# First batches of TensorE written out by hand, one step less between down and up products, W1 on two DMA queues

## The chip, the cores and the metric

The kernel runs on one core of a Trainium2 chip. The metric is device time in microseconds (us) of one execution. Three runs of the kernel before gave 326.95, 327.93 and 328.11 us, median 327.93.

A core has five engines that run side by side and wait for each other through semaphores: TensorE (PE; its weight loads are shown apart as PEld), VectorE (DVE), ScalarE (ACT), GpSimd (POOL) and SyncE (SP), which here only issues DMAs. Each engine takes its instructions in the order of its own list.

## What is computed

128 batches of a 128 x 512 float32 matrix `x[b]`, each with a language id that picks one of ten sets of weights. In the reference, cut to what matters (`_L0_cond_ref` gets `x` as `hidden_states` and the ids as `language_ids`):

```python
w1 = W1[language_ids]; w2 = W2[language_ids]        # (512,128) and (128,512) of each batch
h = relu(einsum('bsh,bha->bsa', hidden_states, w1) + b1[language_ids][:, None, :])
adapted = einsum('bsa,bah->bsh', h, w2) + b2[language_ids][:, None, :]
x = hidden_states + adapted
mean = jnp.mean(x, axis=-1, keepdims=True)
var = jnp.mean(jnp.square(x - mean), axis=-1, keepdims=True)
normed = (x - mean) * rsqrt(var + 1e-5)
return normed * gamma[language_ids][:, None, :] + beta[language_ids][:, None, :]
# and the result is the original x plus this
```

## The kernel before

**Start.** All ten W1, all ten W2 and the rows of beta, gamma and b2 are loaded once. SP issues, in this order: the ids, gamma, the first half of x group 0 (`load_part(0, 2)`, L83), four slices of W1 (L93, 640 KB each, `k` in 0..3), the second half of x group 0, W2 in two halves (L98), and x groups 1 and 2 (L67, `load_x`; a group is four batches, 1 MB). ACT issues beta, b2 and b1.

The thirty rows (ten each of beta, gamma, b2) must stand on all 128 partitions. `spread(r)` does one row: a TensorE product (L155) that picks row `r` out of three stacked bf16 parts into a PSUM buffer of pool `p_y`, and a copy (about 0.6 us) out of it, on ACT where `r % 3 == 2` (L158) and on DVE otherwise (L160). The pool `p_y` has five buffers, used in turn, and the up products take theirs from it too.

**A batch** passes through these functions: `transpose_x` (PE, four 128 x 128 transposes into the single buffer of `p_x`, L191), `copy_xT` (ACT, L195), `stage_w1` (ACT copies the batch's W1 so that TensorE can read it at a fixed address, L186), `down` (PE, four products into the single buffer of `p_h`, L214), `relu` (ACT, L222, reads `p_h`), `up` (PE, L231, with one more product, L230, that adds b2 where `b2_by_matmul`), `residual` (DVE, L237), `negative_mean` (DVE), `square` and `deviation` (ACT), `rstd_1` to `rstd_5`, `scale` and `finish` (DVE, L281 and L290), `store` (SP). POOL prepares `x + b2` (`add_b2`, L201) and `x + beta` (`add_beta`, L208).

**Order.** `keep` ties each engine's instructions to the order in which the program calls them, so the order is written out by hand: one loop over steps `i`. Step `i` has the transposes of batch `i`, the down product of `i-1`, the up product of `i-U` and the residual of `i-U-1`. U is 3. The first `F = U+1 = 4` steps also issue 7 or 8 spreads each, after the step's down product, and hold back the up products; at step 4 come `down(3)`, `up(0)` and `up(1)` ahead of the transposes of batch 4. Fourteen products on a tile of ones (`idle`, L307) stand ahead of everything on TensorE.

`lid` loads the ids of a group of four batches into an engine's registers (L168) when it is first called for that group and engine. At the end of a step it is called ahead for a coming batch.

Of the kernel before, what the change touches and what calls it, by code (L numbers as in the profile page):

```python
# [8 lines left out]
FP = mybir.dt.float32  # L9
BF = mybir.dt.bfloat16  # L10
I32 = mybir.dt.int32
AF = mybir.ActivationFunctionType
# [4 lines left out]
P = 128  # L17
G = 4
EPS = 1e-5
U = 3  # L20


@with_exitstack
def cond_resid_kernel(ctx: ExitStack, tc: tile.TileContext, x, itok, W1, b1, W2, b2, gamma, beta, out):
# [8 lines left out]
    nc = tc.nc  # L33
    B, S, H = x.shape
    L, _, A = W1.shape
# [7 lines left out]
    def keep(ins):  # L43

        engine = ins.ins.engine
        if engine in last:
            tc.add_manual_dep(ins.ins, last[engine], behind, reason="kept order")
        last[engine] = ins.ins.name
        return ins

    const = ctx.enter_context(tc.tile_pool(name="const", bufs=1))
# [6 lines left out]
    p_x = ctx.enter_context(tc.tile_pool(name="p_x", bufs=1, space=PSUM))  # L58
    p_h = ctx.enter_context(tc.tile_pool(name="p_h", bufs=1, space=PSUM))
    p_s = ctx.enter_context(tc.tile_pool(name="p_s", bufs=1, space=PSUM))  # L60
# [4 lines left out]
    def load_x(g):  # L65
        t = xp.tile([P, G, H], FP, tag="x", name=f"x_{g}")
        keep(nc.sync.dma_start(out=t, in_=x[g * G : (g + 1) * G].rearrange("b s h -> s b h")))  # L67
        xs[g] = t

    def xb(b):  # L70
        return xs[b // G][:, b % G, :]
# [5 lines left out]
    w1 = const.tile([P, L, KC, A], FP, name="w1")  # L77
# [4 lines left out]
    def load_part(lo, hi):  # L82
        keep(nc.sync.dma_start(out=x_0[:, lo:hi, :], in_=x[lo:hi].rearrange("b s h -> s b h")))  # L83
# [4 lines left out]
    keep(nc.scalar.dma_start(out=rows[2 * L : 3 * L, :], in_=b2))  # L88
    load_part(0, 2)
    keep(nc.scalar.dma_start(out=b1r, in_=b1))  # L90
    for k in range(KC):
        keep(
            nc.sync.dma_start(out=w1[:, :, k, :], in_=W1[:, k * P : (k + 1) * P, :].rearrange("l p a -> p l a"))  # L93
        )
    load_part(2, G)
    for l in range(0, L, 5):
        keep(
            nc.sync.dma_start(  # L98
                out=w2[:, l * H : (l + 5) * H].rearrange("p (l h) -> p l h", l=5),
                in_=W2[l : l + 5].rearrange("l a h -> a l h"),  # L100
            )
        )
    for g in range(1, 3):
        load_x(g)

    warm = const.tile([P, 1], FP, name="warm")
    nc.vector.memset(warm, 1.0)
    keep(nc.scalar.activation(warm, warm, AF.Sqrt))

    ident = const.tile([P, P], FP, name="ident")  # L110
    make_identity(nc, ident)
# [2 lines left out]
    ones = const.tile([P, P], BF, name="ones")  # L114
# [10 lines left out]
    R = 3 * L  # L125
# [15 lines left out]
    def transpose_b1():  # L141
        b1p = p_h.tile([P, P], FP, tag="h", name="b1p")
        keep(nc.tensor.transpose(b1p[:, :L], b1r, ident[:L, :L]))
        keep(nc.vector.tensor_copy(b1T, b1p[:, :L]))
# [3 lines left out]
    gamma_b = const.tile([P, L * H], FP, name="gamma_b")  # L148
    b2_b = const.tile([P, L * H], FP, name="b2_b")

    def spread(r):
        t = (beta_b, gamma_b, b2_b)[r // L]
        row = p_y.tile([P, H], FP, tag="y", name=f"row_{r}")
        pick_r = pick[:, r : r + 1].to_broadcast([96, P])
        keep(nc.tensor.matmul(row, lhsT=pick_r, rhs=parts[:96, :], start=True, stop=True))  # L155
        dst = t[:, r % L * H : (r % L + 1) * H]
        if r % 3 == 2:
            keep(nc.scalar.copy(dst, row))  # L158
        else:
            keep(nc.vector.tensor_copy(dst, row))  # L160

    lids, xT, w1s, hT, rs, os, ys, ssqs, nmeans, rstds = {}, {}, {}, {}, {}, {}, {}, {}, {}, {}
    phs, pxs, sums = {}, {}, {}

    def lid(b, engine):
        g = b // G
        if (g, engine) not in lids:
            loads, vals = nc.values_load_multi_w_load_instructions(  # L168
                lang[0:1, g * G : (g + 1) * G],
                engines=[engine],  # L170
                min_val=0,
                max_val=L - 1,
                skip_runtime_bounds_check_because="clamped on the chip to 0..L-1 above",
            )
            for ins in loads:
                keep(ins)
            lids[g, engine] = vals
        return lids[g, engine][b % G]

    def b2_by_matmul(b):  # L180
        return b < 4 or b % 4 == 1

    def stage_w1(b):
        w1s[b] = wp.tile([P, KC, A], FP, tag="w1s", name=f"w1s_{b}")
        src = w1.rearrange("p l k a -> p (l k a)")[:, bass.ds(lid(b, ET.Activation) * (KC * A), KC * A)]
        keep(nc.scalar.copy(w1s[b].rearrange("p k a -> p (k a)"), src))  # L186

    def transpose_x(b):
        pxs[b] = p_x.tile([P, KC, P], FP, tag="xT", name=f"pxT_{b}")
        for k in range(KC):  # L190
            keep(nc.tensor.transpose(pxs[b][:, k, :], xb(b)[:, k * P : (k + 1) * P], ident))  # L191

    def copy_xT(b):
        xT[b] = tp.tile([P, KC, P], FP, tag="xT", name=f"xT_{b}")
        keep(nc.scalar.copy(xT[b], pxs.pop(b)))  # L195
# [14 lines left out]
    def down(b):  # L210
        phs[b] = p_h.tile([P, P], FP, tag="h", name=f"ph_{b}")
        for k in range(KC):
            keep(
                nc.tensor.matmul(  # L214
                    phs[b], lhsT=w1s[b][:, k, :], rhs=xT[b][:, k, :], start=(k == 0), stop=(k == KC - 1)
                )
            )
        del xT[b], w1s[b]

    def relu(b):  # L220
        hT[b] = tp.tile([P, P], FP, tag="hT", name=f"hT_{b}", bufs=6)
        keep(nc.scalar.activation(hT[b], phs.pop(b), AF.Relu, bias=b1T[:, bass.ds(lid(b, ET.Activation), 1)]))  # L222

    def up(b):
        v = lid(b, ET.PE)
        ys[b] = p_y.tile([P, H], FP, tag="y", name=f"py_{b}")
        m = b2_by_matmul(b)
        if m:
            pick_b = pick[:, bass.ds(v + 2 * L, 1)].to_broadcast([96, P])
            keep(nc.tensor.matmul(ys[b], lhsT=pick_b, rhs=parts[:96, :], start=True, stop=False))  # L230
        keep(nc.tensor.matmul(ys[b], lhsT=hT[b], rhs=w2[:, bass.ds(v * H, H)], start=not m, stop=True))  # L231
        del hT[b]
# [29 lines left out]
    def rstd_2(g):  # L262
        y0s[g] = st.tile([P, 2], FP, tag="y0", name=f"y0_{g}")
        keep(nc.vector.reciprocal(y0s[g], sds.pop(g)))
# [32 lines left out]
    def on(b):  # L297
        return 0 <= b < B
# [3 lines left out]
        nc.sync.dma_start(out=out[b], in_=os[g][:, j, :])  # L302


    idle = p_x.tile([P, H], FP, tag="xT", name="idle")
    for _ in range(14):
        keep(nc.tensor.matmul(idle, lhsT=ones, rhs=ones[:, 0:1].to_broadcast([P, H]), start=True, stop=True))  # L307

    F = U + 1
    for i in range(B + U + 7):  # L310
        if i < B and i % G == 0 and i // G + 3 < NG:
            load_x(i // G + 3)
        b = i - U - 1
        if i == F:
            down(i - 1)
            up(0)
            up(1)
        if on(i):
            transpose_x(i)
        if i == 0:  # L320
            transpose_b1()
        if on(b + 2):
            add_b2(b + 2)
        if on(b):
            add_beta(b)
        if on(i - 1) and i != F:
            down(i - 1)
        if on(i):
            copy_xT(i)
        if i < F:  # L330
            if on(i - 1):
                relu(i - 1)
            for r in range(i * R // F, (i + 1) * R // F):
                spread(r)
            if i == 0:
                stage_w1(0)
            stage_w1(i + 1)
        else:
            if on(i + 1):
                stage_w1(i + 1)  # L340
            if on(i - 1):
                relu(i - 1)
        if i > F and on(i - U):
            up(i - U)


        g, half = divmod(b, 2)
        p = g - 1
        mine, old = 0 <= p < B // 2, 0 <= p - 1 < B // 2
        if half == 0:  # L350
            if on(b):
                residual(b)
            if mine:
                scale(2 * p)
            if on(b):
                negative_mean(b)
            if mine:
                rstd_1(p)
                rstd_2(p)
            if old:  # L360
                finish(2 * p - 1)
                if p < B // 2:
                    store(p - 1)
                else:
                    store_half(B - 1)
            if mine:
                rstd_3(p)
        else:
            if on(b):
                residual(b)  # L370
            if mine:
                rstd_4(p)
                scale(2 * p + 1)
                rstd_5(p)
            if on(b):
                negative_mean(b)
            if mine:
                finish(2 * p)
                if p == B // 2 - 1:
                    store_half(B - 2)  # L380
        if on(b):
            square(b)
            if half == 1:
                deviation(g)

        for n, engine in ((i + 3, ET.Activation), (i - U + 3, ET.PE), (b + 1, ET.DVE), (b + 5, ET.Pool)):
            if on(n):
                lid(n, engine)
# [37 lines left out]
```

## Time and profile before

| | |
|---|---|
| median of three runs | 327.93 us |
| the profiled execution | 327.5 us |
| its span, first to last instruction | 325.7 us |
| PE, DVE, ACT, POOL busy | 304.6, 301.5, 283.6, 274.7 us |
| mean granted TensorE clock | 0.972 |
| bytes moved by DMA | 72.88 MB |

The profiled execution lasted 1.8 us longer than its span, and lies 0.4 us under the median. Busy times are of records that overlap a little where an engine is pipelined, so a stage with "40.00 of 40.00" says that no gap is seen, not that the engine could do no more. A timeline line gives the start, the length, the engine and line, and in brackets the idle time ahead of it with what ended it.

### The profile page before, as it was taken

The page shows a single profiled execution, that of the slowest core. Times are in us where ns is not written, and L with a number is a line of the kernel's source. Part 1 is how long each engine was busy: PE and PEld are TensorE (multiplying, and loading weights), DVE is VectorE, ACT ScalarE, POOL GpSimd, SP SyncE. Part 2 cuts the span into 40 slices and gives each one's busy share as a digit, 9 for nine tenths or more (in the row PEclk, how much of TensorE's full clock was granted, in tenths as well). Part 3 has the DMA queues.
Part 4 walks back from the last instruction along what each step waited for, and adds up shares of the span by engine and source line. Part 5 has one row for each costly group of instructions (what it writes and reads, how often), then busy time and mean ns, then how long its engine had stood idle before and what let it go on. Part 6 is the DMA issues. An engine that isn't in the chain of part 4 may idle for free. (4 is left out here: it accounts for less than half of the span.)

```text
span 325.7 us, 7127 instructions
## 1 busy us (share of the span) xinstructions
PE 304.6 (94%) x1872; PEld 225.4 (69%) x1872; DVE 301.5 (93%) x993; ACT 283.6 (87%) x716; POOL 274.7 (84%) x229
## 2 busy tenths in 40 slices
PE   8298999999999999999999999999999999999940
PEld 3255777877777777777777787777777877777710
DVE  6267699999999999999999999999999999999995
ACT  3266999999999999999999999999999999999940
POOL 1034989999999999999999999999999999999910
PEclk9679999999999999999999999999999999999995
DMA  7996296666666777766666667777666666733323
GB/s 209 322 387 252 48 332 222 223 219 225 233 244 224 236 258 262 253 213 214 208 233 241 235 223 255 259 251 237 222 220 222 230 232 227 233 132 130 129 115 144
DMA packets 40954, 72.88 MB, mean 224 GB/s; under 512 B 1705, under 2 KB 6836, under 8 KB 40914
## 3 DMA queue, kind: packets, MB, share of 16 engines
q1 hardware_dynamic: 40854, 72.38, 66.0%
q8 instruction: 15, 0.25, 0.3%
q14 instruction: 25, 0.20, 0.2%
q10 hardware_dynamic: 60, 0.05, 0.1%
HBM read 38.86 MB, written 33.55 MB: 222 GB/s over the span
## 5 line engine op out<-in xcount | busy, mean ns | idle before, releaser
L208 POOL TENSOR_TENSOR o<-x,beta_b 128x512 f32<-128x512 f32 x128 | 162.0, 1278 | 17.6 <-DVE beta_b L160 17.6
L214 PE MATMUL ph<-xT,w1s 128*128 128x128 f32 x1024 | 136.4, 276 | 5.8 <-ACT w1s L186 5.6
L201 POOL TENSOR_TENSOR r<-x,b_b 128x512 f32<-128x512 f32 x93 | 118.8, 1277 | 17.3 <-DVE py L237 10.1
L231 PE MATMUL py<-w,hT 128*128 x256 | 131.2, 594 | 1.9 <-ACT sq L249 1.3
L214 PEld LDWEIGHTS ph<-xT,w1s 128*128 128x128 f32 x1024 | 125.4, 193 | 7.1 <-ACT w1s L186 5.9
L191 PEld LDWEIGHTS pxT<-ident,x 128*128 128x128 f32 x512 | 64.0, 141 | 68.3 <-issue 41.2
L281 DVE SCALAR_TENSOR_TENSOR py<-py,nmean,gamma_b 128x512 f32<-128x512 f32 x128 | 96.2, 751 | 0.0
L290 DVE SCALAR_TENSOR_TENSOR o<-py,rstd,o 128x512 f32<-128x512 f32 x128 | 94.7, 740 | 1.5 <-issue 0.4
L249 ACT ACTIVATE sq<-py,nmean 128x512 f32<-128x512 f32 x128 | 88.4, 690 | 5.5 <-DVE nmean L242 5.0
L195 ACT COPY xT<-pxT 128x512 f32<-128x512 f32 x128 | 74.6, 583 | 14.2 <-PE pxT L191 10.3
L186 ACT COPY w1s<-w 128x512 f32 x128 | 80.0, 626 | 5.5 <-DMA w<-in_L_cond_W_dram 5.5
L191 PE MATMUL pxT<-ident,x 128*128 128x128 f32 x512 | 77.3, 274 | 1.0 <-ACT xT L195 0.7
L237 DVE SCALAR_TENSOR_TENSOR py<-py,r 128x512 f32<-128x512 f32 x93 | 64.5, 694 | 2.4 <-PE pxT L191 0.7
L222 ACT ACTIVATE hT<-ph,b1T 128x128 f32<-128x128 f32 x128 | 48.1, 376 | 2.0 <-PE ph L214 1.9
L231 PEld LDWEIGHTS py<-w,hT 128*128 128x128 f32 x256 | 41.6, 192 | 5.2 <-ACT sq L249 2.1
L237 DVE SCALAR_TENSOR_TENSOR py<-py,x 128x512 f32<-128x512 f32 x35 | 24.2, 692 | 4.7 <-PE py L231 3.9
L249 ACT ACTIVATION_READ_ACCUMULATOR sq<-py,nmean 128x1 f32 x128 | 26.3, 205 | 0.0
L255 ACT ACTIVATE sd<-ssq,eps 128x2 f32<-128x2 f32 x64 | 18.9, 296 | 2.1
L242 DVE TENSOR_SCALAR nmean<-sum 128x1 f32<-128x1 f32 x128 | 18.7, 146 | 0.1
L230 PE MATMUL py<-parts,pick 96*128 96x512 bf16 x35 | 13.3, 381 | 0.0
L270 DVE TENSOR_TENSOR stat<-stat,y 128x2 f32<-128x2 f32 x64 | 13.2, 206 | 0.0
L237 DVE DVE_READ_ACCUMULATOR py<-py,r 128x1 f32 x93 | 13.1, 141 | 0.0
(41 smaller groups left out, 92.7 us busy)
## 6 DMA issues: line engine op xcount, KB each, us to landing
out_dram<-o SPq DMA_DIRECT2D x63, 512.0 KB, 3.5
x<-in_x_dram SPq DMA_DIRECT2D x31, 1024.0 KB, 6.1
w<-in_L_cond_W_dram SPq DMA_DIRECT2D x4, 640.0 KB, 6.3
w<-in_L_cond_W_dram SPq DMA_DIRECT2D x2, 1280.0 KB, 11.4
x<-in_x_dram SPq DMA_DIRECT2D x2, 512.0 KB, 3.6
out_dram<-o SPq DMA_DIRECT2D x2, 256.0 KB, 2.1
rows<-in_L_cond_beta_dram ACTq DMA_DIRECT2D x1, 20.0 KB
rows<-in_L_cond_gamma_dram SPq DMA_DIRECT2D x1, 20.0 KB
```

Source lines behind the costliest of these rows:

```text
L186: keep(nc.scalar.copy(w1s[b].rearrange("p k a -> p (k a)"), src))
L191: keep(nc.tensor.transpose(pxs[b][:, k, :], xb(b)[:, k * P : (k + 1) * P], ident))
L195: keep(nc.scalar.copy(xT[b], pxs.pop(b)))
L201: keep(nc.gpsimd.tensor_tensor(rs[b], xb(b), b2_b[:, bass.ds(v * H, H)], ALU.add))
L208: keep(nc.gpsimd.tensor_tensor(os[g][:, j, :], xb(b), beta_b[:, bass.ds(v * H, H)], ALU.add))
L214: nc.tensor.matmul(phs[b], lhsT=w1s[b][:, k, :], rhs=xT[b][:, k, :], start=(k == 0), stop=(k == KC - 1))
L222: keep(nc.scalar.activation(hT[b], phs.pop(b), AF.Relu, bias=b1T[:, bass.ds(lid(b, ET.Activation), 1)]))
L231: keep(nc.tensor.matmul(ys[b], lhsT=hT[b], rhs=w2[:, bass.ds(v * H, H)], start=not m, stop=True))
L237: keep(nc.vector.scalar_tensor_tensor(ys[b], ys[b], 1.0, r, ALU.mult, ALU.add, accum_out=s))
L249: keep(nc.scalar.activation(sq, ys[b], AF.Square, bias=nmeans[b], accum_out=ssqs[g][:, j : j + 1]))
L281: nc.vector.scalar_tensor_tensor(ys[b], ys[b], nmeans.pop(b), gamma_b[:, bass.ds(v * H, H)], ALU.add, ALU.mult)
L290: nc.vector.scalar_tensor_tensor(o, ys.pop(b), rstds[g][:, j : j + 1], o, ALU.mult, ALU.add)
```

## The change

1. U goes from 3 to 2: the up product of batch `b` is issued in step `b+2`, and with it all that follows a batch, one step sooner after its transposes.
2. The slices `k` = 2 and 3 of W1 are issued by ACT, behind its table load and a small activation, which now come first on it; SP issues `k` = 0 and 1.
3. x group 3 is loaded with groups 1 and 2; before, step 0 of the loop issued it, at the same place of SP's order.
4. TensorE's first four batches are written out ahead of the loop, which now begins at step 3. The order on TensorE is: 12 products on ones (14 before); the transposes of batch 0; rows 0 to 5; the transposes of batch 1; rows 6 to 21, each followed by a half-width product on ones (`spin(1, H // 2)`, 16 in all); four full-width ones; then `down(0)`, transposes of 2, rows 22 to 24, `down(1)`, transposes of 3, rows 25 to 27, `down(2)`, rows 28 and 29, `up(0)`, `up(1)`, `down(3)`, `up(2)`, transposes of 4. Before, it was: transposes of 0, seven rows, transposes of 1, `down(0)`, eight rows, transposes of 2, `down(1)`, seven rows, transposes of 3, `down(2)`, eight rows, `down(3)`, `up(0)`, `up(1)`, transposes of 4.
5. The products on ones write a tile of pool `p_s` and no longer one of `p_x`.
6. Rows 22 to 29 are all copied by DVE: 7 row copies on ACT and 23 on DVE, where it was 10 and 20. `stage_w1(0)` and `stage_w1(1)` stand on ACT behind all seven.

```diff
-U = 3
+U = 2
...
+    warm = const.tile([P, 1], FP, name="warm")
+    nc.vector.memset(warm, 1.0)
+    keep(nc.scalar.activation(warm, warm, AF.Sqrt))
     for k in range(KC):
+        queue = nc.sync if k < 2 else nc.scalar
         keep(
-            nc.sync.dma_start(out=w1[:, :, k, :], in_=W1[:, k * P : (k + 1) * P, :].rearrange("l p a -> p l a"))
+            queue.dma_start(out=w1[:, :, k, :], in_=W1[:, k * P : (k + 1) * P, :].rearrange("l p a -> p l a"))
         )
...
-    for g in range(1, 3):
+    for g in range(1, 4):
         load_x(g)
-
-    warm = const.tile([P, 1], FP, name="warm")
-    nc.vector.memset(warm, 1.0)
-    keep(nc.scalar.activation(warm, warm, AF.Sqrt))
...
-    def spread(r):
+    def spread(r, copier):
...
-        if r % 3 == 2:
+        if copier is nc.scalar:
...
-    idle = p_x.tile([P, H], FP, tag="xT", name="idle")
-    for _ in range(14):
-        keep(nc.tensor.matmul(idle, lhsT=ones, rhs=ones[:, 0:1].to_broadcast([P, H]), start=True, stop=True))
-
-    F = U + 1
-    for i in range(B + U + 7):
+    def spin(n, width):
+        idle = p_s.tile([P, H], FP, tag="s", name="idle")
+        for _ in range(n):
+            keep(
+                nc.tensor.matmul(
+                    idle[:, :width], lhsT=ones, rhs=ones[:, 0:1].to_broadcast([P, width]), start=True, stop=True
+                )
+            )
+
+
+    spin(12, H)
+    transpose_x(0)
+    transpose_b1()
+    copy_xT(0)
+    for r in range(22):
+        spread(r, nc.scalar if r % 3 == 2 else nc.vector)
+        if r == 5:
+            transpose_x(1)
+            copy_xT(1)
+        elif r > 5:
+            spin(1, H // 2)
+    stage_w1(0)
+    stage_w1(1)
+    spin(4, H)
+    for b in range(3):
+        down(b)
+        if b < 2:
+            transpose_x(b + 2)
+        relu(b)
+        if b < 2:
+            copy_xT(b + 2)
+        for r in range(22 + 3 * b, min(25 + 3 * b, R)):
+            spread(r, nc.vector)
+        stage_w1(b + 2)
+    up(0)
+    up(1)
+    down(3)
+    relu(3)
+    stage_w1(5)
+
+    for i in range(3, B + U + 7):
...
-        if i == F:
-            down(i - 1)
-            up(0)
-            up(1)
-        if on(i):
+        if i == 4:
+            up(2)
+        if i > 3 and on(i):
             transpose_x(i)
...
-        if on(i - 1) and i != F:
+        if i > 4 and on(i - 1):
             down(i - 1)
-        if on(i):
+        if i > 3 and on(i):
             copy_xT(i)
-        if i < F:
...
+        if i > 4 and on(i + 1):
             stage_w1(i + 1)
-        else:
...
-        if i > F and on(i - U):
+        if i > 4 and on(i - 1):
+            relu(i - 1)
+        if i > 4 and on(i - U):
             up(i - U)
```

More of the change, by code (lines that the diff above doesn't have):

```diff
@@ L313, in cond_resid_kernel @@
         b = i - U - 1
-        if i == F:
-            down(i - 1)
-            up(0)
-            up(1)
-        if on(i):
+        if i == 4:
+            up(2)
+        if i > 3 and on(i):
             transpose_x(i)
-        if i == 0:
-            transpose_b1()
         if on(b + 2):
@@ L325, in cond_resid_kernel @@
             add_beta(b)
-        if on(i - 1) and i != F:
+        if i > 4 and on(i - 1):
             down(i - 1)
-        if on(i):
+        if i > 3 and on(i):
             copy_xT(i)
-        if i < F:
[L331 to L336, printed above, removed]
-            stage_w1(i + 1)
-        else:
[L339 to L342, printed above, removed]
-        if i > F and on(i - U):
+        if i > 4 and on(i + 1):
+            stage_w1(i + 1)
+        if i > 4 and on(i - 1):
+            relu(i - 1)
+        if i > 4 and on(i - U):
             up(i - U)
```

## The prediction

> **What bounds the kernel now.** First the busy time of each engine by stage (windows view; columns in the header line):
>
> ```profile
> core 0: us, PE busy (x) PEld busy (x) DVE busy (x) ACT busy (x) POOL busy (x), PEclk, DMA share, GB/s
> 40.00:80.00 40.00, 40.00 (x254) 30.30 (x254) 39.65 (x136) 38.26 (x99) 37.98 (x31) 1.00 0.73 247
> ...
> 280.00:310.00 30.00, 30.00 (x192) 22.77 (x190) 29.76 (x100) 28.41 (x74) 29.22 (x24) 1.00 0.36 141
> ```
>
> From 40 us to 310 us TensorE has no gap, at full clock. DVE is close behind. In the PE timeline the transposes of batch 6 start at 34.35 and those of batch 127 at 306.25: 271.90 / 121 = 2.247 us a batch. DVE alone, once TensorE is done, takes 2.21 (residuals at 311.12 and 315.54, two batches apart). So TensorE sets the pace and DVE has 0.04 us a batch to spare. What is won before the steady stretch is carried to the end if TensorE and DVE both get it. The tail is DVE's: `residual(124)` starts at 308.94, right after `up(124)`, and DVE then hardly stops until 322.16.
>
> The start is different (PE timeline; batches are told apart by the order of the list):
>
> ```profile
> 1.17 4.50 PE L307 MATMUL idle<-ones 128*128 128x512 bf16 x14 [1.17 <-POOL ones L115]
> ...
> 8.56 0.63 PE L191 MATMUL pxT<-ident,x 128*128 128x128 f32 x4 [0.20 <-PE row L155]
> 14.82 2.08 PE L214 MATMUL ph<-xT,w1s 128*128 128x128 f32 x8 [5.63 <-ACT w1s L186]
> 16.69 3.62 PE L155 MATMUL row<-parts,pick 96*128 96x512 bf16 x8
> ...
> 30.15 0.60 PE L191 MATMUL pxT<-ident,x 128*128 128x128 f32 x4
> 31.48 0.65 PE L191 MATMUL pxT<-ident,x 128*128 128x128 f32 x4 [0.73 <-ACT xT L195]
> ...
> 35.90 1.02 PE L231 MATMUL py<-w,hT 128*128 x2
> ```
>
> TensorE stands still for 5.63 us for the W1 copy of `down(0)`, and then is slow: that product takes 2.08 us where it takes 1.06 later, eight rows 3.62 where later 2.13. The windows view says why:
>
> ```profile
> 10.00:12.00 2.00, 0.00 (x0) 0.00 (x0) 0.00 (x0) 0.00 (x0) 0.00 (x0) 0.66 1.20 290
> 12.00:14.00 2.00, 0.00 (x0) 0.00 (x0) 0.00 (x0) 0.00 (x0) 0.00 (x0) 0.50 1.16 307
> ...
> 16.00:18.00 2.00, 2.00 (x9) 1.11 (x8) 0.64 (x1) 0.58 (x2) 0.00 (x0) 0.50 1.05 388
> ...
> 22.00:24.00 2.00, 1.78 (x9) 0.82 (x8) 1.76 (x3) 1.56 (x4) 0.00 (x0) 1.00 1.04 386
> ```
>
> From 10 us to almost 21 us the granted clock is half. And while TensorE, DVE and ACT all stand still (10 to 14 us), 23 of the 30 rows are yet to be spread. ACT and SP show what they wait for:
>
> ```profile
> 14.15 1.14 ACT L186 COPY w1s<-w 128x512 f32 x2 [5.48 <-DMA w<-in_L_cond_W_dram]
> ```
>
> ```profile
> 1.95 6.11 SPq L93 DMA_DIRECT2D w<-in_L_cond_W_dram x4
> 8.11 2.20 SPq L83 DMA_DIRECT2D x<-in_x_dram x1
> 10.35 1.65 SPq L98 DMA_DIRECT2D w<-in_L_cond_W_dram x2
> ```
>
> W1 lands just before 14.15. The landing records put the W2 halves at 18.66 and 22.22 and x group 1 at 24.75. Last, DVE gets its third up product late, 3.31 us after it could take it:
>
> ```profile
> 34.60 0.70 DVE L237 SCALAR_TENSOR_TENSOR py<-py,x 128x512 f32<-128x512 f32 x1 [3.31 <-PE py L231]
> ```
>
> [...] idle from 9.1, half clock from about 10.6, full again near 20.9. [...] Before, W1 moves at 290 to 307 GB/s with a DMA share of 1.16 to 1.20: the engines are full[...]; two queues are not shown before. [...]
>
> **The change part by part**, against the profiled 327.5 us (span 325.7).
>
> *W1 on two queues: 0.* The 2.62 MB lie behind the same full engines. ACT issues at about 3.6 (its activation ends at 3.56); SP's first two issues took 0.46 and 0.66 us, so ACT is free near 4.8, ahead of its first copy at about 5.9. Bounds: if two queues raised the rate to the 387 GB/s of the later stretch, W1 would land 2 us sooner; if ACT's slices only get short turns beside SP's x and W2, up to 2 us later; if ACT is held in issuing as SP was on its third slice (2.67 us), all ACT's copies slip by 1 to 2 us. W2 and x follow the same sum of bytes, so 22.2 and 24.75 stay. x group 3 keeps its place on SP.
>
> *Rows ahead of `down(0)`.* Of rows 0 to 21 DVE copies 15, at 0.62 us (five took 3.08), from 6.92 on: to 16.2. ACT copies seven in its shadow. A row's product needs the buffer of the row five before it, so row 20 is issued when row 15, DVE's 11th, is out: 6.92 + 11 x 0.62 = 13.7; ACT copies it by 14.8. TensorE's own pace, a row (0.25) and a half-width product (estimate 0.15, from half of 0.22 and its load), is 1.2 us per three rows against DVE's 1.24: even. Row 21 is out at about 14.5, the four full products end at 15.5. `stage_w1(0)` runs on ACT from 14.8, W1 being there. So `down(0)` starts at 15.5 to 16.5 (before: 14.82), at full clock, with 22 rows done and not 7. The 28 products on ones that stand behind or between rows cost nothing while DVE's copies or W1 cover them; uncovered, about 1 us. Two fewer at the head: 0.4 us, covered by DVE's preparation of the rows (first row at 6.5).
>
> *From `down(0)` to the transposes of 4*, from starts in the timeline at full clock: down 0.90, transposes 0.43, row 0.25, up with b2 1.08. Down, transposes, three rows, twice: 4.2. `down(2)` and two rows: 1.4. That gives `up(0)` at 21.1 or later, but W2's second half is only there at 22.2: its second product starts near 22.3 and ends at 23.2. This wait is the new limit. Behind it on TensorE stand `up(1)` 1.08, `down(3)` 0.90, `up(2)` 1.08, with a load of ids into registers ahead of the last (0.33): the transposes of 4 start at 26.2 to 26.6 (before: 30.15), just after x group 1.
>
> *Then ACT.* It has `relu(3)`, `stage_w1(5)` and `square(0)` ahead of `copy_xT(4)`, so that copy ends near 27.4, and the transposes of 5 start at 27.5 to 28 (before: 31.48, with the same wait). `down(4)` and `up(3)` follow: `up(3)` ends near 30. Before it ended at 36.76. **Gain about 6.8**, of which 1.3 (transposes and a down product) come from U, as up products no longer stand behind one more batch.
>
> *U = 2 in the steady stretch: 0.* `up(i-2)` stands right behind `down(i-1)`, which writes the single `p_h` buffer and so waits for `relu(i-2)` already. Around 46 us, relu ended at 45.88, the next down started at 46.17, and an up there starts at 47.06: 1.2 us after its relu. Up to residual, square and copies keep their distance in steps. Bounds: nothing below, 0.05 us a batch above.
>
> *Others.* `add_b2` on POOL waits for the last b2 row (28.76 before, about 22.5 now), so POOL keeps its lead. Three more copies on DVE: 1.9 us, in time in which it waited. In the tail each up product comes as early against DVE as before, so nothing is given back there.
>
> Sum: 6.8, less 0.3 for ACT and register loads that I can't place: 6.5. 327.5 - 6.5 = 321.0; the median of the runs is 0.4 above the profiled one: **321.3 us**.
>
> **Rivals.**
> A. *As above*: 319.6 to 323.2 (gain 4.7 to 8.3 against the median). For it: every wait that goes stands on the path of TensorE and DVE.
> B. *The start slips*: W1 late by 2 us on ACT's queue, ACT held in issuing, or rows and ones slower on TensorE than DVE's copies. `down(0)` at 18 and the transposes of 4 at 28.5: gain 4 or less, 323.2 to 326.3. Against it: W1's engines are full either way.
> C. *No change*: the early start is eaten by another engine, say POOL (274.7 us busy; 2.13 a batch against 2.247) or DVE (2.21). Both have slack, so 327 to 328.5 needs an unseen wait.
> D. *Slower*: with U = 2 TensorE waits for relu in each step.
>
> ```profile
> PEld ph L214 <- ACT hT L222: 0.8, 2, 0.4
> ```
>
> In the list of waits (engine, releaser: total us, times, longest) this wait came twice. If ACT falls behind by the 1.2 us of room, TensorE stalls every batch; from 6.5 / 124 = 0.052 us a batch it eats the gain, and at 0.1 us it gives 321.3 + 12.4 = 333.7. Against it: ACT is idle for about 0.10 us a batch (38.26 busy of 40, 17.8 batches), and the down product meets the same relu first.
> E. *Two queues do nothing for W1*: included in A.
>
> **How the numbers follow.** A 0.79, B 0.13, C 0.04, D 0.04. A's own range with a part of B's gives 319.5 to 323.6. About 0.5%, 1.6 us, can be told from no change here: faster than 326.3 are A and nearly all of B, 0.91; same 0.05; slower 0.04.
>
> **What would show it.** Clock 1.00 through the first 30 us; no idle of 5 us ahead of the first down product; that product at 15.5 to 16.5; W1 landing near 14; the first up waiting for W2 near 22.2; the transposes of 4 at 26.2 to 27; the steady stretch still 2.25 us a batch. Wrong if W1 lands past 16, if a batch takes over 2.27 us, or if DVE or POOL shows a regular wait on TensorE that was not there.

## The result and the profile after

The changed kernel takes 323.54 us (median of 4 runs, 322.53 to 324.68) where the kernel before took 327.76 (4 runs): ratio 0.9876, 95% interval 0.983 to 0.9921. That is a gain of 1.2%, clear of the spread, but about three fifths of the forecast one: 321.3 of 327.93 would be 0.980. Further rounds gave 323.67 us and 0.988 (0.9846 to 0.9914). The first median lies just inside the upper end of the forecast range (319.5 to 323.6), the second just outside. The profiled execution took 324.36 us, one of the two slower of the four, with a span of 322.5, 3.2 us less than the span before.

The steady stretch and the end are as they were (windows view after; same columns as shown of before):

```profile
core 0: us, PE busy (x) PEld busy (x) DVE busy (x) ACT busy (x) POOL busy (x), PEclk, DMA share, GB/s
...
40.00:80.00 40.00, 40.00 (x257) 30.58 (x256) 39.68 (x133) 38.12 (x99) 39.38 (x33) 1.00 0.72 242
...
280.00:310.00 30.00, 29.53 (x183) 21.76 (x182) 29.75 (x103) 27.24 (x72) 26.00 (x21) 1.00 0.32 122
```

The start is not what was forecast. TensorE after:

```profile
14.52 1.36 PE L310 MATMUL idle<-ones 128*128 128x256 bf16 x4
18.83 2.08 PE L215 MATMUL ph<-xT,w1s 128*128 128x128 f32 x8 [2.95 <-ACT w1s L187]
20.70 1.06 PE L192 MATMUL pxT<-ident,x 128*128 128x128 f32 x4
...
29.84 0.60 PE L192 MATMUL pxT<-ident,x 128*128 128x128 f32 x4
31.11 0.66 PE L192 MATMUL pxT<-ident,x 128*128 128x128 f32 x4 [0.68 <-ACT xT L196]
...
32.72 1.02 PE L232 MATMUL py<-w,hT 128*128 x2
33.58 0.60 PE L192 MATMUL pxT<-ident,x 128*128 128x128 f32 x4
```

The rows are done as planned, row 21 at 14.3. But then TensorE again stands still for the W1 copy, and `down(0)` starts at 18.83, 4 us later than before and 2.3 us past the end of what was forecast. It takes 2.08 us, as before, at half clock (PEclk 0.51 from 20 to 22 us, in the windows view below). The transposes of 4 come at 29.84, only 0.3 us sooner than before. Behind them the shorter order gains: `up(3)`, the product at 32.72, is out by 33.58, where before it was out at 36.76. These 3.2 us are the gain in span. The windows view shows the stall:

```profile
16.00:18.00 2.00, 0.00 (x0) 0.00 (x0) 0.11 (x1) 0.00 (x0) 0.00 (x0) 1.00 1.07 374
18.00:20.00 2.00, 1.17 (x5) 1.17 (x6) 0.00 (x0) 1.14 (x2) 0.00 (x0) 0.64 1.05 385
20.00:22.00 2.00, 2.00 (x11) 1.66 (x10) 0.00 (x0) 0.52 (x2) 0.00 (x0) 0.51 1.05 387
```

From 16 to 18 us TensorE and ACT do nothing, and the DMA engines are full (share 1.07, 374 GB/s). ACT says what they wait for, and the list of DMA issues has the times to landing; it counts only the first of the two slices of each queue:

```profile
18.16 1.14 ACT L187 COPY w1s<-w 128x512 f32 x2 [3.19 <-DMA w<-in_L_cond_W_dram]
```

```profile
w<-in_L_cond_W_dram SPq DMA_DIRECT2D x2, 640.0 KB, 7.0
w<-in_L_cond_W_dram ACTq DMA_DIRECT2D x2, 640.0 KB, 9.3
```

By the landing records, SP's two slices of W1 landed at 8.9 and 13.7 us, ACT's at 11.5 and 18.1. It is ACT's second slice that everything waits for. Before, the last slice had landed near 14.1. The trace's DMA packets, counted by queue and by the time at which they end, show how that comes:

```
             SP's queue               ACT's queue
8 to 12 us   1122 packets, 512 B      1139 packets, 512 B   (144 and 146 GB/s)
13 to 15 us   277 packets, 2048 B      296 packets, 512 B   (284 and  76 GB/s)
```

The two queues get nearly equal numbers of packets, with 512 bytes on both (1122 and 1139) as with 2048 beside 512 (277 and 296), and so in every tenth of a microsecond from 13 to 15 us: 12 to 15 of SP's and 12 to 17 of ACT's. Counts as even as these fit queues that are served in turn, packet by packet. While both carry W1, each gets half of the bytes (144 and 146 GB/s). From 12 us on SP's queue comes to x and W2, whose packets of 2048 bytes are four times as large, and ACT's slice falls to 76 GB/s.

### The profile page after: what moved, and what is told of

The parts are those of the page before. It is cut to its first block, busy times and chain, and to the rows that moved or that the text cites. A ratio compares the mean times of both kernels' runs of the same rounds, so it can differ in the third digit from the quotient of the medians.

```text
span 322.5 us, 7159 instructions
## 1 busy us (share of the span) xinstructions
PE 305.1 (95%) x1889; PEld 227.0 (70%) x1890; DVE 303.8 (94%) x996; ACT 280.6 (87%) x713; POOL 274.7 (85%) x229
## 5 line engine op out<-in xcount | busy, mean ns | idle before, releaser
L196 ACT COPY xT<-pxT 128x512 f32<-128x512 f32 x128 | 73.8, 577 | 14.6 <-PE pxT L192 12.2
L223 ACT ACTIVATE hT<-ph,b1T 128x128 f32<-128x128 f32 x128 | 47.4, 371 | 6.1 <-PE ph L215 6.1
L250 ACT ACTIVATION_READ_ACCUMULATOR sq<-py,nmean 128x1 f32 x128 | 26.4, 206 | 0.0
## 6 DMA issues: line engine op xcount, KB each, us to landing
w<-in_L_cond_W_dram SPq DMA_DIRECT2D x2, 1280.0 KB, 15.9
```

Source lines behind the costliest of these rows:

```text
L250: keep(nc.scalar.activation(sq, ys[b], AF.Square, bias=nmeans[b], accum_out=ssqs[g][:, j : j + 1]))
```

## The experiments

Each ratio is that of a kernel's time to the kernel before's, in the same rounds.

**All W1 on SP.**

```diff
-        queue = nc.sync if k < 2 else nc.scalar
+        queue = nc.sync
```

> The changed kernel with all four W1 slices on SP again. Theory 1 (turns): the engines take the two queues' packets one for one, so ACT's 512-byte packets of W1 fall to a quarter of the bytes as soon as SP's queue has 2048-byte packets of x and W2; that put the last slice at 18.0 us. On one queue W1 lands near 14.1, down(0) starts near 15.6 at full clock, the transposes of 4 near 26.5 (29.9 in the changed kernel), and the time falls by about 3.3 us, to 320 or 321. Rival (W2 and ACT bound the start anyway, W1's delay is hidden): the transposes of 4 stay within 0.5 us of 29.9 and the time within 0.5 us of the changed kernel.

Measured: 321.9 us against 327.25, ratio 0.9864 (0.9836 to 0.9891); span 319.5, 3.0 less than the changed kernel's. TensorE's timeline:

```profile
16.41 1.16 PE L215 MATMUL ph<-xT,w1s 128*128 128x128 f32 x8
...
22.45 1.10 PE L232 MATMUL py<-w,hT 128*128 x2 [0.27 <-DMA w<-in_L_cond_W_dram]
...
26.43 0.60 PE L192 MATMUL pxT<-ident,x 128*128 128x128 f32 x4
27.70 0.66 PE L192 MATMUL pxT<-ident,x 128*128 128x128 f32 x4 [0.68 <-ACT xT L196]
```

This is the forecast timetable: `down(0)` at 16.4 with no stall worth listing ahead of it, the first up product waiting for W2 until 22.45, the transposes of 4 and 5 at 26.4 and 27.7. So the profile bears out the theory of turns. But the profiled execution is the fastest of six, and that of the changed kernel one of the slower of its four. In the medians the gap is 1.1 to 1.5 us and not the 3.3 expected, and the intervals of the two ratios overlap: two of the six executions took 324 us. They weren't profiled, so why stays open.

**The kernel before with W1 on two queues**, and nothing else:

```diff
+        queue = nc.sync if k < 2 else nc.scalar
         keep(
-            nc.sync.dma_start(out=w1[:, :, k, :], in_=W1[:, k * P : (k + 1) * P, :].rearrange("l p a -> p l a"))
+            queue.dma_start(out=w1[:, :, k, :], in_=W1[:, k * P : (k + 1) * P, :].rearrange("l p a -> p l a"))
```

> The kernel before with this edit alone: W1 slices 2 and 3 issued by ACT. Theory 1 (turns): the last slice lands near 18, down(0) moves from 14.8 to about 18.8, and the time rises by 3 to 5 us, to 331 to 333. Rival (two queues cost or bring nothing, as the prediction had it): W1 lands near 14, time within 0.5 us of the kernel before.

Measured: 330.94 us, ratio 1.0115 (1.0095 to 1.0136). ACT's timeline has the copy of W1 at 17.78, where it stood at 14.15:

```profile
17.78 1.14 ACT L187 COPY w1s<-w 128x512 f32 x2 [7.80 <-DMA w<-in_L_cond_W_dram]
```

So this edit alone makes the kernel before slower by 1.2%, 3.7 us, clear of noise and as the theory of turns had it. ACT had stood idle for 7.80 us by then, so it was the landing that counted and not the time that ACT spends on issuing. The prediction's "0" for it is wrong.

**Three slices on SP, one on ACT.**

```diff
-        queue = nc.sync if k < 2 else nc.scalar
+        queue = nc.sync if k < 3 else nc.scalar
```

> The changed kernel with three W1 slices on SP and one on ACT. By the theory of turns ACT's slice (1280 packets of 512 bytes) gets half of the 290 GB/s from about 6 us and is done near 10.5 us, before SP reaches its 2048-byte packets of x and W2; W1 lands near 14, and the time is that of all four on SP, 321 to 322 us. Rival (a second queue for W1 costs in itself, by ACT's issues or the mixing): W1 past 15 and 323 us or more.

Measured: 321.61 us against 327.01, ratio 0.983 (0.9815 to 0.9845); ACT's slice is through soon after 10 us (19 of its packets end later), `down(0)` starts at 15.9, the transposes of 4 at 26.35. The W1 copy no longer waits for W1:

```profile
15.23 1.14 ACT L187 COPY w1s<-w 128x512 f32 x2 [0.23 <-DVE gamma_b L161]
```

The second queue costs nothing that these runs show. What costs is that its slices are still under way when the other queue comes to larger packets. The five executions lie within 0.4 us, so this run also gives the best measure of the loss in the times: 0.983 against the changed kernel's 0.9876 and 0.988, some 1.6 us, though the intervals overlap for the first of these and only just part for the second.

**More products on ones ahead of `down(0)`** in the changed kernel, to part the half clock from the lateness:

```diff
-    spin(4, H)
+    spin(16, H)
```

> The changed kernel with sixteen full-width products on ones ahead of down(0) where there were four: they run from 14.5 to about 18.2, so TensorE isn't idle when W1 comes. If the half clock from 18.5 to 22.0 is a part of the loss, down(0) takes 1.06 and not 2.08 us, and the transposes of 4 come about 1.5 us sooner (28.4), the time 1.5 us below the changed kernel. Rival (only the lateness of W1 counts): no more than 0.3 us.

Measured:

```profile
18.88 1.16 PE L215 MATMUL ph<-xT,w1s 128*128 128x128 f32 x8
...
28.39 0.60 PE L192 MATMUL pxT<-ident,x 128*128 128x128 f32 x4
```

`down(0)` is as late as in the changed kernel, but takes 1.16 us, at clock 1.00 (windows view); the transposes of 4 stand at 28.39 instead of 29.84; span 321.03 instead of 322.47. So between the profiled executions the half clock cost 1.4 us, and the lateness of W1 the other 1.6 (321.03 to 319.48). The time, 322.83 us and 0.9866 (0.9848 to 0.9885), can't be told from the changed kernel's, so the 1.4 us are shown by profiles alone. The lateness is there in the times too: W1 on three slices and one gave 0.983 with an interval that ends at 0.9845, some 1.2 us less. The four executions here lie within 0.3 us, where those of the changed kernel lie 2 us apart.

**U = 3**, first in the changed kernel, then with all W1 on SP:

```diff
-U = 2
+U = 3
...
-        if i == 4:
-            up(2)
```

> The changed kernel with U = 3: up products again three steps behind the transposes, the written-out start kept except that up(2) goes back into step 5. If U is worth what the prediction said, a transpose and a down product, the time rises by 1.3 us against the changed kernel. Rival (U shortens nothing, since TensorE does the same work in all): within 0.4 us.

Measured: 326.17 us, 0.9961 (0.9944 to 0.9978), span 326.3. More than either theory allowed, and not due to U alone: in its profiled execution, the slowest of fifteen, W1 came another 1.1 us later and the half clock lasted 6.8 us, not 3.4. As a measure of U it is inconclusive.

> All W1 on SP, and U = 3. Set against W1 on SP with U = 2: if U is worth a transpose and a down product, the span is 1.3 us longer (320.8) and the time 322.5 to 323.5 us. Rival 1 (U shortens nothing): within 0.4 us. Rival 2, raised by the run of the changed kernel with U = 3, whose span was 3.9 us longer: U is worth more, 2.5 us or more.

Measured: 323.34 us against 327.01, 0.9897 (0.9869 to 0.9924); span 321.3 against 319.5 with U = 2. U is worth 1.8 us of span between these two profiles, more than the 1.3 forecast and less than rival 2's 2.5. The times differ by 1.1 us (0.9897 against 0.9864) and their intervals overlap. The timeline shows where the rest can come from:

```profile
22.72 1.10 PE L232 MATMUL py<-w,hT 128*128 x2 [1.40 <-DMA w<-in_L_cond_W_dram]
...
26.34 0.63 PE L192 MATMUL pxT<-ident,x 128*128 128x128 f32 x4 [0.56 <-DMA x<-in_x_dram]
```

With `up(2)` moved behind the transposes of 4, these don't start sooner, as one would think from its 1.08 us. They wait for x group 1 until 26.34. With U = 2, `up(2)` stands in time that would be lost to that wait (what goes with the late x group 1 is said below, at `down(3)`).

**No ones between the rows**, with all W1 on SP:

```diff
-        elif r > 5:
-            spin(1, H // 2)
...
-    spin(4, H)
```

> All W1 on SP, and the twenty products on ones between the rows and ahead of down(0) left out (the twelve at the head stay). Theory (rows alone, some 0.22 of each 0.41 us, keep the clock up[...]): the clock stays at 1.00 and the time is that of W1 on SP within 0.5 us. Rival (the ones hold the clock): half clock for 3.4 us or more at about 12 to 20 us, and 1 to 2 us longer.

Measured: 321.63 us, 0.982 (0.9803 to 0.9837), no slower than W1 on SP, as the theory had it, but not for its reason: the clock did halve, from 16.8 to 20.2 us, as the rival had it. Neither is right in full. The windows view:

```profile
12.00:14.00 2.00, 1.09 (x5) 0.29 (x4) 2.00 (x4) 1.17 (x2) 2.00 (x2) 1.00 1.16 312
14.00:16.00 2.00, 0.81 (x3) 0.19 (x2) 2.00 (x5) 1.13 (x3) 0.46 (x1) 1.00 1.04 384
16.00:18.00 2.00, 1.88 (x11) 1.88 (x12) 0.60 (x2) 0.96 (x3) 0.00 (x0) 0.71 1.06 388
18.00:20.00 2.00, 2.00 (x9) 1.30 (x8) 1.09 (x2) 1.10 (x2) 0.00 (x0) 0.50 1.05 386
```

The transposes of 4 come 0.86 us later (27.29), the span is only 0.4 longer (319.9). So the start with ones gives about half of its lead back later, and in the times the twenty ones bring nothing that can be seen. The list of waits of the kernel with W1 on SP shows, between 40 and 72 us:

```profile
DVE py L238 <- POOL r L202: 0.5, 1, 0.5
```

That wait is neither in the list of the changed kernel for that stretch nor in that of the kernel without ones. With W1 on SP, TensorE and DVE start so early that they catch up with POOL, whose first b2 sum needs a batch of x group 1:

```profile
26.27 1.27 POOL L202 TENSOR_TENSOR r<-x,b_b 128x512 f32<-128x512 f32 x1 [11.75 <-DMA x<-in_x_dram]
```

**`down(3)` ahead of the first up products**, with all W1 on SP:

```diff
+    down(3)
+    relu(3)
+    stage_w1(5)
     up(0)
     up(1)
-    down(3)
-    relu(3)
-    stage_w1(5)
```

> All W1 on SP, and down(3), relu(3), stage_w1(5) ahead of up(0), up(1). With W1 on SP up(0) waits for W2 (22.3); down(3) takes 0.9 us and needs nothing of W2, so it fits ahead of it: the transposes of 4 about 0.7 us sooner (25.5), and the time 0.7 us below W1 on SP. Rival (down(3) has to wait for ACT, or T4 and T5 are then bound by x group 1 or ACT): within 0.3 us.

Measured: 321.34 us, 0.9819 (0.9805 to 0.9834); the transposes of 4 at 26.30, 0.13 us sooner, and the span is the same 319.5. The median lies 0.6 us under that of W1 on SP, but that one had two executions near 324 us. By the profile the rival was right:

```profile
26.30 0.63 PE L192 MATMUL pxT<-ident,x 128*128 128x128 f32 x4 [0.50 <-DMA x<-in_x_dram]
```

Taking away the wait for W2 shows one for x group 1. That wait is longer than it need be. The landing of x group 1 is reported in sixteen parts; here fifteen had come by 25.1 and the last at 26.16, while in the kernel before all had come by 24.93. A 16384-byte packet of the instruction queue (`q8` in the list of DMA queues) goes with it:

```
                                     that packet ends     x group 1 complete
before                               30.7 us              24.93 us
no ones between the rows             28.9                 25.32
changed kernel                       27.2                 25.63
W1 on SP                             23.5                 26.11
down(3) ahead                        22.7                 26.16
U = 3 with W1 on SP                  22.7                 26.21
```

In all five profiles with the packet between 21 and 24 us and x group 1 in one piece it is complete at 26.1 to 26.2, in all six with the packet later at 24.9 to 25.6. That the packet is the cause isn't tested. With x there at 24.9, the transposes of 4 could have followed `up(2)` at 25.64 here (estimate: its start, 24.78, and 0.86).

**x group 1 in two halves**, on top of that:

```diff
-    for g in range(1, 4):
+    x_1 = xp.tile([P, G, H], FP, tag="x", name="x_1")
+    xs[1] = x_1
+    for lo in (0, 2):
+        keep(nc.sync.dma_start(out=x_1[:, lo : lo + 2, :], in_=x[G + lo : G + lo + 2].rearrange("b s h -> s b h")))
+    for g in range(2, 4):
         load_x(g)
```

> All W1 on SP, down(3) ahead of up(0), and x group 1 in two DMAs of two batches. With down(3) ahead, the transposes of 4 waited for x group 1 (26.3), and so did POOL's first b2 sum. Half a group is there about 1.3 us sooner: the transposes of 4 near 25.6, POOL's first b2 sum near 25.0, and the time 0.7 to 1.2 us below that of down(3) ahead (relative to the kernel before: 0.979 where it was 0.982). Rival (ACT or W2 bounds there anyway): within 0.3 us.

Measured: 320.71 us against 327.57, 0.979 (0.9771 to 0.9809); the transposes of 4 at 25.69, right behind `up(2)`, and POOL's first sum at 24.95, still behind x but 1.4 us sooner; span 318.4.

```profile
24.95 1.27 POOL L206 TENSOR_TENSOR r<-x,b_b 128x512 f32<-128x512 f32 x1 [11.08 <-DMA x<-in_x_dram]
```

This is the best version of the study, 2.1% below the kernel before, as expected; its interval and that of the version before it just overlap.

**The changed kernel once more.**

> The changed kernel once more, to see what its spread of 322.5 to 324.7 us comes from. Theory (clock): TensorE idles some 3 us ahead of down(0)[...], so that in some executions a half-clock stretch follows (324.4, as profiled: 18.5 to 22.0 us) and in others none or a short one; the executions fall into two groups about 1.8 us apart, and a profile of the fast group shows no half clock ahead of the tail. Rival (W1's last slice lands earlier or later): the groups differ in the landing, at an equal clock.

Measured: 323.67 us, 0.988; executions from 322.04 to 325.86, not in two groups. The profiled one (324.34) again had half clock, from 18.8 to 22.2, behind 3.03 us of idle TensorE. No execution of the fast end was profiled, so what the spread comes from stays open. That the kernel with sixteen ones hardly spreads speaks for the clock; that W1's copy came anywhere from 17.8 to 19.3 us in the five profiles with two slices on ACT speaks for the landing. Neither is shown.

## Why the prediction was right or wrong

- **The step that failed: "W1 on two queues: 0".** The prediction said that the bytes "lie behind the same full engines". The rates fit that: from 8 to 12 us the two queues together moved 290 and 291 GB/s, one queue in the kernel before 291 and 290 (windows view by 2 us). But the sum of the rates doesn't say how the queues share it. By the counts they were served in turn (277 packets against 296 in 2 us), and a packet was a single row, 2048 bytes of x or W2 against 512 of W1, so that SP's queue got 284 GB/s and ACT's 76. The sum left that out. The prediction had the mechanism in its bounds ("ACT's slices only get short turns beside SP's x and W2"), with up to 2 us, and gave no working for these 2 us. With turns supposed, which the trace before doesn't show, the rate could have been estimated from it: 387 GB/s is 189 packets of 2048 bytes a us, 290 GB/s is 566 of 512; taken in turn that is 142 of each, 73 GB/s for ACT. With the 0.38 MB that ACT's slices had left at 12 us (counted in the trace after) that makes 5.2 us, to 17.2; the last packet ended at 17.44. Measured: W1 4 us later, `down(0)` at 18.83 instead of 15.5 to 16.5, and with it a half clock. Put together, 3.0 us of span between profiles: 1.6 for the lateness and 1.4 for the clock. In the times it is some 1.6 us (0.988 against 0.983).
- **"Clock 1.00 through the first 30 us"** failed for the same reason. The four full products kept TensorE busy until 15.9 us and not until 18.8. Nor did the trace before speak for a full clock across a gap like this: there the clock halved 1.5 us after TensorE had gone idle (9.19 to 10.65), here 2.7 us after (15.88 to 18.55).
- **The rest of the sum held, within 1 us.** With W1 on SP, `down(0)` (16.4), the wait for W2 (22.45), the transposes of 4 (26.4) and of 5 (27.7) are those forecast, and the span of the profiled execution, the fastest of six, fell by 6.2 us where the sum had 6.5. The missing 0.3 is in line with the 0.5 us that POOL held DVE up: from the transposes of 6 to those of 127 TensorE took 272.10 us there, and 271.62 in the changed kernel. In the times, the versions with W1 out of the way (0.983 with three slices on SP) stay about 1 us short of the forecast 0.980.
- **"POOL keeps its lead"** was only half right. In the changed kernel POOL's first b2 sum waits for the last b2 row, as forecast, but at 27.37 and not near 22.5, which cost nothing that the trace shows. With W1 on SP it waits for x group 1 instead, until 26.27, and the lead is gone (0.5 us). "22.2 and 24.75 stay" held for W2 and not for x group 1, which was complete at 26.11 there.
- **U.** Right in sign and place; 1.3 us forecast, 1.8 between two profiles with W1 on SP, where `up(2)` fills a wait for x.
- **Steady stretch at no cost.** Right: with both U the down products are 2.19 or 2.41 us apart (without and with the b2 product), and rival D's wait for relu comes once, with 0.2 us.
- **Of the rivals**, B happened: a slipping start through ACT's queue, with `down(0)` past 18. The measured 323.54 us lie in B's range and outside A's own (319.6 to 323.2); the range given in the end reached 323.6 only by its part of B. The argument against B was "W1's engines are full either way", which says nothing on who gets them. C and D did not happen.
- **Two small misreadings that changed nothing.** ACT issued its slices at 2.17 us, beside its table load, and not at 3.6. The landings before were at 18.84 (first half of W2) and 24.93 (x group 1), 0.2 us later than read.

## What to carry to other kernels

Before a transfer that others wait for is moved to a second DMA queue, look at what stands behind it on the first: the queues shared the engines packet for packet here, so small packets lost to large ones (76 against 284 GB/s). Split it so that the second queue is empty before the first comes to large packets (three slices and one: 0.983 here), or leave it on one (0.9864). And when a start is bound by transfers, take the landing time of every tensor in it: behind the wait for W1 stood one for W2, and behind that one for x group 1, so that taking away the wait for W2 alone brought the transposes of 4 only 0.13 us.

## What the runs showed of the hardware

- Changed kernel: from 8 to 12 us two queues with packets of 512 bytes got 280 and 285 packets per us; from 13 to 15 us, with 2048-byte packets on one of them, 139 (2048 bytes) and 148 (512 bytes).
- The clock halved 2.7 us into an idle stretch of TensorE of 2.95 us (changed kernel, at 18.55), and 1.5 us into one in the kernel before (at 10.65). With no ones it halved at 16.8, after short rows, 0.8 to 1.1 us of work in 2 us, and 1.31 us of idle at the end. The half-clock stretches of the start lasted 3.4 us (changed kernel), 6.8 (U = 3) or 10.2 (before).
- In the five profiles where a 16384-byte packet of the instruction queue ended between 21 and 24 us, the last of the sixteen parts of x group 1 came at 26.1 to 26.2, 1.0 to 1.3 us behind the fifteenth.
